# Attention scores by blocks of keys: one merged list of 64x64 matmuls, split additions, and a reordered head of the cycle

## The chip, the cores and the metric

The kernel runs on 1 core of one Trainium2 chip. Times are device microseconds of one execution of the whole program. Before the change three runs gave a median of 1027.56 us (1027.11 to 1027.65).

## What is computed

There are B = 64 sequences of N = 128 tokens with 512 channels. Each goes through one attention layer with 16 query heads of 64 channels that share one head of keys and values, with a bias per head, a causal mask, a mask of valid keys and an extra null key; then an output projection, a layer norm, and the residual. Cut to what matters:

```python
xn = layernorm(x, g_in)
q = (xn @ Wq).reshape(b, n, H, DH).transpose(0, 2, 1, 3) * scale    # 16 heads of 64
k, v = split(xn @ Wkv)                                              # one head, plus a null key
sim = jnp.einsum('bhid,bjd->bhij', q, k) + bias
sim = jnp.where(causal_mask, neg, sim)      # query i sees the null key and the keys up to i
sim = jnp.where(mask_p, sim, neg)
out = jnp.einsum('bhij,bjd->bhid', jax.nn.softmax(sim), v)
y = x + layernorm(out.reshape(b, n, INNER) @ Wo, g_out)
```

All of it is in float32. Each float32 matmul shows as two records of loading weights and two of multiplying (two passes) in the trace.

## The kernel before, in words

**Stages and order.** The order of the work on all engines is written out by hand: a prologue, then `cycle(c)` for c = 1 to 29, then a tail. A cycle handles two sequences in each of several stages at once: for b0 = 2c and b1 = 2c+1 the softmax, for two later ones (by n0 = b0+2 and n1 = b0+3) the scores, for the two before (p = b0-2) the output projection. It also makes the queries of a later group of four sequences (`q_one`, `leaf`: products of a fast matrix multiplication whose parts are added in place), the keys and values (`kv_mm`), and norms. Each cycle ends with `region(c)` (L1057): the scores of n0 and n1, and then the weighted values of b0 and b1.

**Scores.** The 128 queries of a sequence are four blocks of 32. For all 16 heads, the rows of a score tile are 128 = 2 blocks x 2 sets of heads x 32 queries. The lower half (`hf` = 0) has blocks 0 and 1 and a row of 64 keys, the upper half (`hf` = 1) blocks 3 and 2 and a row of 128 keys. `heads` (L645) makes them of 64x64 matmuls, four at a time in the four quarters of TensorE: r is the half of the contracted rows (heads with even or odd number), i the half of the output rows (i = 0: block 0, or 3 in the upper half; i = 1: block 1, or 2). So one half with index i of the array does blocks 0 and 3, and the other one blocks 1 and 2. The weights of each matmul are 64 queries (64 columns), and the keys stream through: 64 in the lower half, 128 in the upper one, for both blocks alike, though block 0 needs only 32, block 1 64, block 2 96 and block 3 128. The causal mask does away with the rest.

**Banks.** The upper half of n0 goes to the PSUM tile `s` (`ps_s`), the lower halves of both to `a` and `c`, and the upper half of n1 to two `w` banks. The values of `region` use `s` again, with `X` and `Y`. In the next cycle `q_one(c, 1, 0)` and `q_one(c, 6, 0)` multiply into `a`, `q_one(c, 5, 0)` into `c`, and `leaf(c, 2, 0)` into `w`.

**After the scores.** `scores_add` (L682) adds each piece of scores to the tile `S[b]`, which holds bias and masks already (VectorE, seven additions for a pair: one of 1024 columns, four of 256, two of 512). Then come the maximum (`scores_max`), the exponentials (ScalarE), the sum's reciprocal, and the scaling (GpSimd).

**Head of a cycle.** ScalarE moves the values out of PSUM (`values_out`: pieces 0 and 2 of p, then of p+1, then 1 and 3 of both). `q_one(c, 1, 0)` multiplies into `a` and has ScalarE copy the result (`first_into`, L503); the product of `q_one(c, 6, 0)` adds to the same bank, and so waits for that copy.

Of the kernel before, what the change touches and what calls it, by code (L numbers as in the profile page):

```python
# [17 lines left out]
def kernel(  # L18
# [405 lines left out]
    def q_part(g, c, h):  # L424

        f = c % NF
        return qT[g, f // FH, h][:, f % FH, :, :, c // NF, :]
# [214 lines left out]
    KEYS = LK, UK  # L642
    WITH_NULL = slice(0, 1 + NL), slice(1 + NL, ROW)

    def heads(b, hf, to):  # L645
        g, t = divmod(b, GB)
        for f in range(NF):
            for r in range(2):
                rows = slice(r * DH, (r + 1) * DH)
                for i in range(2):  # L650
                    nc.tensor.matmul(  # L651
                        to[r][i * DH : (i + 1) * DH, f, :],
                        qT[g, f // FH, t // GH][
                            rows, f % FH, t % GH, NQ - 1 - i if hf else i
                        ],
                        kT[g][rows, 0 : NQ if hf else NQ // 2, t, :],
                        start=True,
                        stop=True,
                    )

    def scores_upper(b, pool, tags):
        if len(tags) == 1:
            ps = pool.tile([P, 2, NF, N], FP, tag=tags, name=f"ps_{b}_1")
            heads(b, 1, [ps[:, r] for r in range(2)])
            pss[b, 1] = [(slice(0, R8), ps)]
        else:
            ps = [pool.tile([P, NF, N], FP, tag=t, name=f"ps_{b}_1{r}") for r, t in enumerate(tags)]
            heads(b, 1, ps)
            pss[b, 1] = [(slice(r * NF, (r + 1) * NF), ps[r]) for r in range(2)]

    def scores_lower(bs):
        low = [
            ps_q.tile([P, 2, NF, NL], FP, tag="ac"[r], name=f"ps_{bs[0]}_0{r}")
            for r in range(2)
        ]
        for k, b in enumerate(bs):
            heads(b, 0, [low[r][:, k] for r in range(2)])
            pss[b, 0] = [(slice(r * NF, (r + 1) * NF), low[r][:, k]) for r in range(2)]

    pss = {}  # L680

    def scores_add(b, hf):  # L682
        for ks, ps in pss.pop((b, hf)):
            sv = S[b][:, ks, KEYS[hf]]
            if ks.stop - ks.start == R8:
                sv = sv.rearrange("p (r f) j -> p r f j", r=2)
            nc.vector.tensor_tensor(sv, ps, sv, ALU.add)  # L687

    def scores_max(b, hf):
        if hf == 0:  # L690
# [289 lines left out]
    def q_one(c, k, h):  # L980
        i = 2 * c + 4 + h
        g, f = divmod(i, GB)
        if g >= NG:
            return
        if k == 1 and f % FH == 0:
            q_tile(g, f // FH)
        if k == 1:
            product(g, f, 1, ps_q, "a")
            if c >= LEAF:
                first_into(g, f, 0)  # L990
            else:
                keep("a", "p1")
        elif k == 2:
            product(g, f, 2, ps_w, "w")
            q_out(g, f, lo_t, "w", "p1")
        elif k == 5:
            product(g, f, 5, ps_q, "c")
        elif k == 6:
            product(g, f, 6, ps_q, "a", start=False)
            if c >= LEAF:  # L1000
                first_into(g, f, 1)
            else:
                keep("a", "u2")
        elif k == 7:
            product(g, f, 7, ps_q, "a", start=False)
            if c >= LEAF:
                first_into(g, HC + f, 0)
                nc.vector.tensor_tensor(
                    q_part(g, HC + f, 1), by_block("c"), q_part(g, HC + f, 0), ALU.add
                )  # L1010
            else:
                keep("a", "u3")
                q_out(g, HC + f, hi_t, "c", "u3")
        elif k == 8:
            o = q_part(g, f, 1)
# [62 lines left out]
    def cycle(c):  # L1078
# [19 lines left out]
            scores_max(b1, 0)  # L1098
            scores_max(b1, 1)
        if pair:  # L1100
            values_out(p + 1, (0, 2))
        if fin:
            pair_pow(r)
        if soft:
# [2 lines left out]
            tokens_in(2)  # L1107
        if first and LEAF <= c and more:
            leaf_sums(c // 2 + 1, 3)
        q_one(c, 1, 0)  # L1110
        if fin:
            pair_nmr(r)
        q_one(c, 5, 0)
# [10 lines left out]
            q_one(c, 2, 0)  # L1124
        if c >= LEAF:
            leaf(c, 2, 0)
        if soft:
            exps(b0, 0, 0, 2)
        q_one(c, 6, 0)
        if soft:  # L1130
            exps(b0, 0, 2, 8)
        out_one(p, 1)
        if c % 2 and n0 < B:
            mask_neg(n0 // GB)
# [6 lines left out]
        q_one(c, 7, 0)  # L1141
        if first and LEAF <= c and more:
            leaf_sums(c // 2 + 1, 4)
        if c >= LEAF:
            q_one(c, 8, 0)
        out_one(p, 2)
        if soft:
            exps(b0, 1, 0, 6)
        if fin:
# [90 lines left out]
        if soft:  # L1240
            scale(b1, 1)
        if c >= LEAF:
            leaf(c, 4, 1)
            q_one(c, 8, 1)
        if c < LEAF:
            q_one(c, 3, 1)
        if soft:
# [393 lines left out]
```

## Time and profile before

| | |
|---|---|
| median of three runs | 1027.56 us |
| span of the profiled execution | 1024.9 us |
| TensorE busy with matmuls | 1013.0 us |
| VectorE busy | 852.5 us |
| GpSimd busy | 788.2 us |
| ScalarE busy | 642.8 us |
| a cycle from scores to scores | 31.03 us |

The time of the profiled execution itself isn't shown; its span is 2.66 us shorter than the median of the runs, and that much is taken to lie around the span in all that follows. In the profile PE is TensorE, PEld its loading of weights, DVE VectorE, ACT ScalarE, POOL GpSimd. A row of groups ends with busy time, mean length of one, and idle time ahead of it; a row in order of time begins with start and length. The granted clock of TensorE was 0.998 of full speed.

### The profile page before, as it was taken

How to read it: one execution, taken by the hardware profiler on the slowest of the kernel's cores; microseconds unless marked ns; L12 is line 12 of the kernel's file. 1: busy time of each engine (PE TensorE's matmuls, PEld its weight loads, DVE VectorE, ACT ScalarE, POOL GpSimd, SP SyncE). 2: the span in 40 equal slices, each digit the busy share in tenths (PEclk: the TensorE clock that was granted, in tenths of full speed). 3: DMA queues.
4: the chain of work that ended last, by engine and by line, in shares of the span. 5: the costliest groups of instructions: out<-in, count | busy, mean ns of one | idle time of the engine just before them, and what ended most of it. 6: DMA issues, size and time to landing. Idle time of an engine off the chain costs nothing. (4 is left out here: it accounts for less than half of the span.)

```text
span 1024.9 us, 31793 instructions
## 1 busy us (share of the span) xinstructions
PE 1013.0 (99%) x12104; PEld 900.7 (88%) x12104; DVE 852.5 (83%) x2000; ACT 642.8 (63%) x2742; POOL 788.2 (77%) x710
## 2 busy tenths in 40 slices
PE   9999999999999999999999999999999999999997
PEld 8888888888888889888889888889888898888876
DVE  6776887888888888888888878788888888878798
ACT  2655776555776556775556765557765567755591
POOL 3799959688696878959689596887968789596874
PEclk9999999999999999999999999999999999999999
DMA  7542350524315152241623505253151521402203
GB/s 212 165 125 55 104 135 26 158 64 135 107 43 152 49 158 84 93 118 32 171 71 106 135 23 158 64 140 101 46 152 46 157 85 73 111 25 67 84 2 104
DMA packets 70264, 100.91 MB, mean 98 GB/s; under 512 B 27744, under 2 KB 31328, under 8 KB 68320
## 3 DMA queue, kind: packets, MB, share of 16 engines
q1 hardware_dynamic: 69008, 97.83, 33.1%
q8 instruction: 96, 1.57, 0.7%
q10 hardware_dynamic: 1104, 1.05, 0.3%
q14 instruction: 56, 0.46, 0.2%
HBM read 63.19 MB, written 33.55 MB: 94 GB/s over the span
## 5 line engine op out<-in xcount | busy, mean ns | idle before, releaser
L701 ACT ACTIVATE s<-s,nmax 128x65 f32<-128x65 f32 (+1 forms) x1024 | 382.2, 413 | 3.5 <-DVE nmax L692 3.5
L701 ACT ACTIVATION_READ_ACCUMULATOR s<-s,nmax 128x1 f32 x1024 | 242.0, 236 | 0.0
L722 POOL TENSOR_TENSOR s<-s,rinv 128x1024 f32<-128x1024 f32 (+1 forms) x128 | 189.4, 1482 | 46.4 <-DVE rinv L718 46.4
L635 POOL TENSOR_TENSOR s<-biasp,mneg 128x1552 f32<-128x1552 f32 x64 | 205.0, 3224 | 2.0 <-DMA x<-in_x_dram 2.0
L810 ACT ACTIVATE oT<-poX,nv 128x256 f32<-128x256 f32 x58 | 27.5, 474 | 219.2 <-PE poX L770 113.0
L687 DVE TENSOR_TENSOR s<-ps,s 128x256 f32<-128x256 f32 (+2 forms) x224 | 120.0, 605 | 15.7 <-PE ps L651 15.2
L556 DVE TENSOR_TENSOR qT<-pl,qT 128x128 f32<-128x128 f32 (+1 forms) x420 | 122.4, 323 | 3.3 <-PE pl L553 3.3
L860 PE MATMUL pyX<-wo,oT 128*128 128x256 f32 x512 | 121.4, 380 | 0.0
L692 DVE TENSOR_REDUCE nmax<-s 128x8 f32<-128x520 f32 (+1 forms) x128 | 116.5, 949 | 0.1
L860 PE MATMUL pyX<-wT,oT 128*128 128x256 f32 x488 | 115.7, 380 | 0.7 <-POOL oT L843 0.7
L737 DVE STREAM_TRANSPOSE sb<-s 128x1536 f32<-128x1536 f32 x64 | 113.1, 1768 | 0.6 <-POOL s L722 0.6
L860 PEld LDWEIGHTS pyX<-wo,oT 128*128 128x128 f32 x512 | 97.0, 190 | 14.3 <-issue 0.9
L917 POOL TENSOR_TENSOR rstdo<-rstdo,nhalf 128x1 f32<-128x1 f32 x64 | 35.0, 548 | 91.5 <-DVE rstdo L913 91.5
L860 PEld LDWEIGHTS pyX<-wT,oT 128*128 128x128 f32 x488 | 88.4, 191 | 10.8 <-POOL oT L843 1.1
L651 PE MATMUL ps<-kT,qT 64*64 64x128 f32 (+1 forms) x4096 | 93.7, 246 | 0.4 <-issue 0.4
L651 PEld LDWEIGHTS ps<-kT,qT 64*64 64x64 f32 x4096 | 85.5, 134 | 5.5 <-issue 2.1
L770 PE MATMUL pos<-sb,vr 32*64 32x128 f32 (+1 forms) x1792 | 81.4, 321 | 0.0
L843 POOL TENSOR_TENSOR yS<-oT 128x512 f32<-128x512 f32 x32 | 40.8, 1274 | 45.4 <-ACT oT L810 42.0
L770 PE MATMUL poY<-sb,vr 32*64 32x128 f32 x720 | 74.6, 348 | 0.0
L770 PE MATMUL poX<-sb,vr 32*64 32x128 f32 x960 | 73.5, 299 | 0.0
L503 ACT COPY qT<-pa 128x256 f32<-128x256 f32 x168 | 68.2, 406 | 1.4 <-PE pa L597 1.4
L331 DVE STREAM_TRANSPOSE xb<-x 128x512 f32<-128x512 f32 x56 | 39.4, 705 | 34.1 <-ACT x L310 34.1
(150 smaller groups left out, 2545.6 us busy)
## 6 DMA issues: line engine op xcount, KB each, us to landing
res<-in_x_dram SPq DMA_DIRECT2D x64, 256.0 KB, 2.9
out_dram<-y SPq DMA_DIRECT2D x58, 256.0 KB, 2.1
x<-in_x_dram SPq DMA_DIRECT2D x224, 64.0 KB, 2.0
xd<-xb SPq DMA_DIRECT2D x14, 1024.0 KB, 4.3
xT<-xd SPq DMA_DIRECT2D x56, 256.0 KB, 5.4
vr<-vd SPq DMA_DIRECT2D x64, 128.0 KB, 3.3
x<-in_x_dram SPq DMA_DIRECT2D x8, 256.0 KB, 4.8
vd<-vt SPq DMA_DIRECT2D x32, 64.0 KB, 6.2
```

What stands on the lines that cost most here:

```text
L503: nc.scalar.copy(q_part(g, c, h), by_block("a"))
L556: nc.vector.tensor_tensor(o, p, o, ALU.add)
L635: nc.gpsimd.tensor_tensor(S[b], biasp, mneg[:, t].unsqueeze(1).broadcast_to([P, R8, ROW]), ALU.add,)
L651: nc.tensor.matmul(to[r][i * DH : (i + 1) * DH, f, :], qT[g, f // FH, t // GH][rows, f % FH, t % GH, NQ - 1 - i if hf else i], kT[g][rows, ...
L687: nc.vector.tensor_tensor(sv, ps, sv, ALU.add)
L692: nc.vector.tensor_reduce(nmax[b][:, hf], S[b][:, :, WITH_NULL[hf]], AX.X, ALU.max, negate=True)
L701: nc.scalar.activation(row, row, AF.Exp, bias=nmax[b][:, hf, k : k + 1], accum_out=rsum[b][:, hf, k : k + 1],)
L722: nc.gpsimd.tensor_tensor(sv, sv, rinvs.pop((b, hf)).unsqueeze(2).broadcast_to([P, R8, sv.shape[2]]), ALU.mult,)
L737: nc.vector.transpose(sb.rearrange("p j e q -> p e j q"), S[b][:, :, 1 : ROW - 1].rearrange("p e (j k) -> p e j k", k=Q),)
L770: nc.tensor.matmul(po[s][rows, half], vr[g][quad(s), j, t, :], sb[quad(s), slots, r * NF : (r + 1) * NF, :], start=start, stop=True, skip_ ...
L843: nc.gpsimd.tensor_tensor(o, l, m, op)
L860: nc.tensor.matmul(prod[key], h[:, c, :], w[:, c, :], start=(start and c == 0), stop=(c == HC - 1), skip_group_check=not start,)
```

## The change

**Scores.** Each block of 32 queries is multiplied with its own keys only: 32, 64, 96 and 128 instead of 64, 64, 128 and 128. The numbers of matmuls and of weight loads stay the same. In `region`, the banks of all four pieces are taken first, and one list for both sequences replaces four loops. `heads` sorts that list by the place that each matmul would begin at if one block of 32 keys took one unit of time, for each index i apart, so that matmuls of both i with different lengths stand beside each other. In the tail the pieces are still made one by one, with the new lengths.

**Additions.** Scores of keys that a block hasn't been multiplied with are no longer there to be added. So each addition is split in two: one over all 128 rows and the keys that both blocks have, one over the 64 rows of the longer block and its last 32 keys. Seven additions of a pair become fourteen, with as many columns in all.

**Head of the cycle.** From cycle 2 on, `q_one(c, 1, 0)`, and with it the copy out of `a`, stands ahead of `values_out(p + 1, (2,))`. The eight exponentials of `exps(b0, 0)` stand together behind `q_one(c, 6, 0)` (before: two ahead of it, six behind). Both additions out of bank `c` (`q_one(c, 7, 0)` and `q_one(c, 8, 0)`) stand behind `out_one(p, 2)`, and `q_one(c, 8, 1)` ahead of `leaf(c, 4, 1)`.

```diff
+    def heads(parts):
+        runs = []
+        for i in range(2):
+            at = 0
+            for b, hf, to in parts:
+                block = NQ - 1 - i if hf else i
+                for f in range(NF):
+                    runs.append((at, i, b, block, f, to))
+                    at += block + 1
+        for _, i, b, block, f, to in sorted(runs, key=lambda run: run[:2]):
+            g, t = divmod(b, GB)
+            for r in range(2):
+                rows = slice(r * DH, (r + 1) * DH)
+                nc.tensor.matmul(
+                    to[r][i * DH : (i + 1) * DH, f, 0 : (block + 1) * Q],
+                    qT[g, f // FH, t // GH][rows, f % FH, t % GH, block],
+                    kT[g][rows, 0 : block + 1, t, :],
+                    start=True,
+                    stop=True,
+                )
...
     def scores_add(b, hf):
+        first = KEYS[hf].start
+        ends = (Q, 2 * Q) if hf == 0 else (3 * Q, 4 * Q)
         for ks, ps in pss.pop((b, hf)):
...
+            for rows, lo, hi in (
+                (slice(0, P), 0, ends[0]),
+                (slice((1 - hf) * DH, (2 - hf) * DH), ends[0], ends[1]),
+            ):
+                sv = S[b][rows, ks, first + lo : first + hi]
...
+                nc.vector.tensor_tensor(sv, pv, sv, ALU.add)
...
     def region(c):
...
-            scores_upper(n0, ps_s, "s")
-            scores_lower((n0, n1))
-            scores_upper(n1, ps_w, "ww")
+            up0 = score_banks(n0, ps_s, "s")
+            low = lower_banks((n0, n1))
+            up1 = score_banks(n1, ps_w, "ww")
+            heads([(n0, 1, up0), (n0, 0, low[0]), (n1, 0, low[1]), (n1, 1, up1)])
...
         if pair:
-            values_out(p + 1, (0, 2))
+            values_out(p + 1, (0,))
+        early = c < LEAF or p < 0
+        if not early:
+            q_one(c, 1, 0)
+        if pair:
+            values_out(p + 1, (2,))
```

The three places that the prediction speaks of, as the built programs have them. On TensorE, the scores of sequences 14 and 15 began like this before (`ps_1` is the upper half of 14, `ps_00` and `ps_01` the lower halves; the sizes are rows x keys, and x8 means eight alike):

```order
L651 MATMUL ps_1_3279<-kT_1883,qT_0_1_2179 64x128 x8
L651 MATMUL ps_1_3279<-kT_1883,qT_1_1_2600 64x128 x8
L651 MATMUL ps_00_3296<-kT_1883,qT_0_1_2179 64x64 x2
L651 MATMUL ps_01_3297<-kT_1883,qT_0_1_2179 64x64 x2
L651 MATMUL ps_00_3296<-kT_1883,qT_0_1_2179 64x64 x2
```

and now begin like this, at the same place:

```order
L679 MATMUL ps_1_3328<-kT_1911,qT_0_1_2205 64x128 x2
L679 MATMUL ps_1_3328<-kT_1911,qT_0_1_2205 64x96 x4
L679 MATMUL ps_1_3328<-kT_1911,qT_0_1_2205 64x128 x2
L679 MATMUL ps_1_3328<-kT_1911,qT_1_1_2638 64x96 x2
L679 MATMUL ps_1_3328<-kT_1911,qT_1_1_2638 64x128 x2
L679 MATMUL ps_1_3328<-kT_1911,qT_1_1_2638 64x96 x2
L679 MATMUL ps_1_3328<-kT_1911,qT_1_1_2638 64x128 x2
L679 MATMUL ps_00_3329<-kT_1911,qT_0_1_2205 64x64
L679 MATMUL ps_01_3330<-kT_1911,qT_0_1_2205 64x64
L679 MATMUL ps_00_3329<-kT_1911,qT_0_1_2205 64x64
L679 MATMUL ps_01_3330<-kT_1911,qT_0_1_2205 64x64
L679 MATMUL ps_00_3329<-kT_1911,qT_0_1_2205 64x32
```

Before, the four quarters took turns with equal lengths. Now a pair (r = 0 and 1) of one index i follows a pair of the other or of the same, and lengths mix; the lower halves begin while block 3 of the upper one still runs.

On ScalarE, the head of cycle 6 was this before (`oT` from `poX`, `poY` and `pos` are pieces of `values_out`, the copy of `pa` is `first_into`):

```order
L810 ACTIVATE oT_2996<-poX_2918,nv_87 128x2x4x32
L810 ACTIVATE oT_2996<-poY_2919,nv_87 128x2x4x32
L810 ACTIVATE oT_3002<-poX_2918,nv_87 128x2x4x32
L810 ACTIVATE oT_3002<-poY_2919,nv_87 128x2x4x32
L503 COPY qT_0_0_3013<-pa_0_1_3015 128x8x32
```

and is this now:

```order
L832 ACTIVATE oT_3045<-poX_2960,nv_87 128x2x4x32
L832 ACTIVATE oT_3045<-poY_2961,nv_87 128x2x4x32
L832 ACTIVATE oT_3051<-poX_2960,nv_87 128x2x4x32
L503 COPY qT_0_0_3053<-pa_0_1_3055 128x8x32
L832 ACTIVATE oT_3051<-poY_2961,nv_87 128x2x4x32
```

The copy of `pa` has moved from the fifth place to the fourth.

On VectorE, the additions for sequence 14 and the first of 15 were:

```order
L687 TENSOR_TENSOR s_3241<-ps_1_3279,s_3241 128x8x128
L687 TENSOR_TENSOR s_3241<-ps_00_3296,s_3241 128x4x64
L687 TENSOR_TENSOR s_3241<-ps_01_3297,s_3241 128x4x64
L687 TENSOR_TENSOR s_3253<-ps_00_3296,s_3253 128x4x64
L687 TENSOR_TENSOR s_3253<-ps_01_3297,s_3253 128x4x64
```

and are now:

```order
L709 TENSOR_TENSOR s_3290<-ps_1_3328,s_3290 128x8x96
L709 TENSOR_TENSOR s_3290<-ps_1_3328,s_3290 64x8x32
L709 TENSOR_TENSOR s_3290<-ps_00_3329,s_3290 128x4x32
L709 TENSOR_TENSOR s_3290<-ps_00_3329,s_3290 64x4x32
L709 TENSOR_TENSOR s_3290<-ps_01_3330,s_3290 128x4x32
L709 TENSOR_TENSOR s_3290<-ps_01_3330,s_3290 64x4x32
```

Each addition has become a wide one and a narrow one, in the old order. The built program has two waits of TensorE for its own earlier matmuls in each cycle that weren't there: at the first values that go into `s`, and at `leaf(c, 2, 0)`.

More of the change, by code (lines that the diff above doesn't have):

```diff
@@ L643, with score_banks, lower_banks @@
     WITH_NULL = slice(0, 1 + NL), slice(1 + NL, ROW)
[L645 to L661, printed above, removed]
+    pss = {}
+    def score_banks(b, pool, tags):
         if len(tags) == 1:
             ps = pool.tile([P, 2, NF, N], FP, tag=tags, name=f"ps_{b}_1")
-            heads(b, 1, [ps[:, r] for r in range(2)])
             pss[b, 1] = [(slice(0, R8), ps)]
[L666 to L671, printed above, removed]
+            return [ps[:, r] for r in range(2)]
+        ps = [pool.tile([P, NF, N], FP, tag=t, name=f"ps_{b}_1{r}") for r, t in enumerate(tags)]
+        pss[b, 1] = [(slice(r * NF, (r + 1) * NF), ps[r]) for r in range(2)]
+        return ps
+    def lower_banks(bs):
         low = [
@@ L1014, in q_one @@
         elif k == 8:
+            nc.vector.tensor_tensor(
+                q_part(g, HC + f, 1), by_block("c"), q_part(g, HC + f, 0), ALU.add
+            )
             o = q_part(g, f, 1)
@@ L1109, in cycle @@
             leaf_sums(c // 2 + 1, 3)
-        q_one(c, 1, 0)
+        if early:
+            q_one(c, 1, 0)
         if fin:
@@ L1242, in cycle @@
         if c >= LEAF:
+            q_one(c, 8, 1)
             leaf(c, 4, 1)
-            q_one(c, 8, 1)
         if c < LEAF:
```

26 lines of the change are left out of this document (13 added, 13 removed).

## The prediction, made before the changed kernel ran

> **What bounds the kernel now.** I read the page's busy times first, then the stretches of one cycle, then single rows.
>
> ```profile
> span 1024.9 us, 31793 instructions
> PE 1013.0 (99%) x12104; PEld 900.7 (88%) x12104; DVE 852.5 (83%) x2000; ACT 642.8 (63%) x2742; POOL 788.2 (77%) x710
> ```
>
> TensorE has work in 99% of the span, so a gain must shorten its own work or a gap in it; other engines matter only where they make it wait. The span lies 2.66 us under the median of 1027.56; I sum against 1024.9 and add 2.66. A measurement of this kernel can tell about 0.2% (2.1 us) from no change. One cycle in three stretches, scores, values and the rest (each row: stretch, its length, TensorE busy and its matmuls, granted clock, DMA share, GB/s):
>
> ```profile
> 499.07:501.91 2.84, 2.84 (x130) 1.00 0.51 119
> 501.91:504.36 2.45, 2.45 (x116) 1.00 0.88 224
> 504.36:530.10 25.74, 25.74 (x145) 1.00 0.40 113
> ```
>
> The change touches the first, and the beginning of the third.
>
> **The scores: fewer keys.** The scores of that cycle again, cut where the rows change from 128 keys to 64 and back (the counts include matmuls that run across an edge):
>
> ```profile
> 499.07:499.99 0.92, 0.92 (x32) 1.00 0.31 80
> 499.99:500.92 0.93, 0.93 (x72) 1.00 0.60 176
> 500.92:501.91 0.99, 0.99 (x46) 1.00 0.61 101
> ```
>
> In the middle each quarter of the array makes 8 matmuls of two passes: 0.93 / 16 = 58 ns a pass. In the first part it makes 8 passes; without the 0.05 us that the first load of weights takes, 0.87 / 8 = 109 ns. What would a pass of 32 or 96 keys take? A plain run of larger matmuls separates streaming from loading:
>
> ```profile
> 519.33 1.89 PE L860 MATMUL pyY<-wT,yS 128*128 128x256 f32 x8
> 521.06 0.39 PE L553 MATMUL pl<-xS,wq 128*128 128x128 f32 x2
> 521.28 0.39 PE L553 MATMUL pl<-xT,wS 128*128 128x128 f32 x2
> ```
>
> From start to start, eight passes of 256 columns take 1.73 us (216 ns each), two of 128 take 0.22 (110): 0.83 ns a column and about 2.5 ns. A pass of 96 keys should take 82 ns. By that, one of 32 takes 29 ns, if nothing else limits it. But each pass has its own load of 64 columns of weights. The loads of the values (also 64 columns) show their length where nothing hides them, behind a drain:
>
> ```profile
> 501.91 0.13 PEld L770 LDWEIGHTS poX<-sb,vr 32*64 32x64 f32 x2 [0.17 <-issue]
> ...
> 501.96 0.14 PEld L770 LDWEIGHTS poX<-sb,vr 32*64 32x64 f32 x2
> ...
> 502.07 0.14 PEld L770 LDWEIGHTS poX<-sb,vr 32*64 32x64 f32 x2
> ```
>
> The second load on the same part of the array starts 0.05 to 0.06 us after the first: a load occupies it that long. The third comes 0.11 later, with the next pass of 128: a load begins when the pass before it begins, and hides behind it. So a pass takes the longer of stream and load, and at 64 keys both are about equal (53 + 2.5 against 55). With 32 keys the load remains. I take **58 ns for a pass of 32 keys**, as for 64; the other end is 29.
>
> Now the sum by index i, since each half of the array has its own chain. For a pair of sequences, i = 0 has 16 passes of block 3 and 16 of block 0: 16 x 109 + 16 x 58 = 2.67 us, before and after alike. i = 1 has 16 of block 2 and 16 of block 1: 16 x 82 + 16 x 58 = 2.24 instead of 2.67. The values need the whole array, so the longer chain counts: **nothing gained**, where 31 merged lists would have given 31 x 0.43 = 13 us if block 0 had been cheap.
>
> By the Trainium skill (TensorEngine Tiling (Array Packing), Instruction Overhead) a matmul of free size 1 takes as long as one of about 60, which here would make 32 keys cost what 64 do, by another mechanism. No run here shows fewer than 64 keys; by that rule the gain is nothing too.
>
> The merged order lets quarters drift apart. In the values, where lengths are mixed as well, they do so freely:
>
> ```profile
> 502.20 0.38 PE L770 MATMUL poY<-sb,vr 32*64 32x256 f32 x2
> ...
> 502.40 0.29 PE L770 MATMUL poX<-sb,vr 32*64 32x128 f32 x2
> ...
> 502.42 0.38 PE L770 MATMUL poY<-sb,vr 32*64 32x256 f32 x2
> ```
>
> The last row is the second pass of the matmul in the first row; the `poX` between them stands behind both in the program and begins before. Still, the values cost 2.45 us, while one part's own chain (12 passes of 109, 4 of 216, 0.05 for the first load, 0.1 for the change of layout, as between 500.92 + 0.87 and 501.91) sums to 2.32: mixing costs up to 0.13 there. For the scores I take 0.016 a list, 31 x 0.016 = **+0.5 us**, between 0 and 0.13 (4.0 us).
>
> **The head of the cycle.** First an odd cycle, then an even one:
>
> ```profile
> 506.19 0.39 PE L553 MATMUL pl<-xT,wq 128*128 128x128 f32 x2
> 506.44 1.13 PE L597 MATMUL pa<-xS,wS 128*128 128x256 f32 x4
> 507.41 1.89 PE L860 MATMUL pyX<-wo,oT 128*128 128x256 f32 x8
> ```
>
> ```profile
> 537.22 0.38 PE L553 MATMUL pl<-xT,wq 128*128 128x128 f32 x2
> 537.57 1.10 PE L597 MATMUL pa<-xS,wS 128*128 128x256 f32 x4
> 538.51 1.68 PE L860 MATMUL pyX<-wo,oT 128*128 128x256 f32 x7
> ```
>
> Two passes of `pl` end at 506.19 + 0.22 = 506.41, but `pa` begins at 506.44; and its four passes take 0.97 to the next row instead of 4 x 0.216 = 0.86, because the first load isn't hidden. Together 0.14 us lost; in the even cycle 0.13 + 0.08 = 0.20. That it is so in every cycle shows in the groups:
>
> ```profile
> L597 PE MATMUL pa<-xS,wq 128*128 128x256 f32 x256 | 65.8, 380 | 0.0
> ...
> L597 PE MATMUL pa<-xS,wS 128*128 128x256 f32 x240 | 64.2, 390 | 0.5 <-ACT qT L503 0.5
> ```
>
> The waiting group (which also has products elsewhere in the cycle) is 10 ns longer in the mean, 240 x 0.010 = 2.4 us, as 14 x 0.10 + 14 x 0.08 would give. What TensorE waits for is on ScalarE:
>
> ```profile
> 505.29 0.47 ACT L810 ACTIVATE oT<-poX,nv 128x256 f32<-128x256 f32 x1
> 505.65 0.48 ACT L810 ACTIVATE oT<-poY,nv 128x256 f32<-128x256 f32 x1
> 506.00 0.39 ACT L503 COPY qT<-pa 128x256 f32<-128x256 f32 x1
> ```
>
> The copy out of `a` ends at 506.39, and `pa` follows 0.05 later. The change puts the copy one place ahead, to 505.65. Its data are there: the product before it in `a` begins at 504.36 and takes 1.13,
>
> ```profile
> 504.36 1.13 PE L597 MATMUL pa<-xT,wq 128*128 128x256 f32 x4
> ```
>
> so it ends at 505.49. The copy then ends at 506.04, ahead of 506.30, where the load for `pa` could start. The wait goes whole; next on this path is only TensorE's own `pl`. In 28 cycles (2 to 29): 14 x 0.14 + 14 x 0.20 = **-4.7 us**. What is displaced, `values_out(p + 1, (2,))`, comes one copy later, and all six pieces and two copies still end where they did. The exponentials that stood ahead of the second copy follow it, with the same work in sum.
>
> **The additions.** VectorE's costs, by size, then the seven of that cycle together:
>
> ```profile
> L687 DVE TENSOR_TENSOR s<-ps,s 128x256 f32<-128x256 f32 x128 | 45.2, 413 | 0.0
> L687 DVE TENSOR_TENSOR s<-ps,s 128x512 f32<-128x512 f32 x64 | 40.8, 678 | 0.0
> L687 DVE TENSOR_TENSOR s<-ps,s 128x1024 f32<-128x1024 f32 x32 | 39.2, 1224 | 15.7 <-PE ps L651 15.2
> ```
>
> ```profile
> 500.32 3.74 DVE L687 TENSOR_TENSOR s<-ps,s 128x1024 f32<-128x1024 f32 x7
> ```
>
> About 1.05 ns a column and 145 ns fixed. The seven sum to 4.23 but take 3.74, so neighbours overlap by 0.08, and a further addition costs 0.065 net. Rows don't matter to an engine that counts columns:
>
> ```profile
> L331 DVE STREAM_TRANSPOSE xb<-x 128x512 f32<-128x512 f32 x56 | 39.4, 705 | 34.1 <-ACT x L310 34.1
> L384 DVE STREAM_TRANSPOSE vt<-kT 64x512 f32<-64x512 f32 x16 | 11.3, 709 | 0.5
> ```
>
> Seven more: +0.45 us a pair, 14 us of VectorE in all. Who waits? The values into `s` need the first addition: it ends at 500.32 + 1.22 = 501.54, now 501.60, and they begin at 501.91. `a` must be free at 504.36; its last reader now ends near 503. The exponentials wait for the maxima:
>
> ```profile
> 504.98 2.42 DVE L692 TENSOR_REDUCE nmax<-s 128x8 f32<-128x520 f32 x3
> 507.69 0.41 ACT L701 ACTIVATE s<-s,nmax 128x65 f32<-128x65 f32 x1
> ```
>
> They end at 507.40, now near 507.85, and ScalarE now gets there near 508.0, behind the second copy. So in the cycles the cover holds, and I count nothing; without it each cycle would lose up to 0.06 at the values (1.8 us). The two added waits on TensorE are for matmuls finished long before, and both instructions wait longer for VectorE anyway; queued behind them are the values and the head's products. In the tail the cover is thin:
>
> ```profile
> 964.00:985.00 21.00, 20.06 (x470) 16.42 (x469) 19.90 (x40) 14.72 (x81) 15.99 (x10) 1.00 0.01 3
> ```
>
> VectorE (the third pair, 19.90) is busy in 95% of it, so its seven further additions count: **+0.4**. The moved additions out of `c` and the leaf cost nothing: `c` is multiplied into again only in the cycle's second half.
>
> **Sum:** -4.7 + 0.5 + 0.4 = -3.8: span 1021.1, time **1023.8 us**.
>
> **Rivals.**
>
> Cheap short keys: a pass of 32 takes 29 ns, because a load is faster than it looks beside others. For: 64 keys could be bound by either. Against: the 0.055 between two loads. The scores then end 0.43 earlier, but the values meet the first addition (501.60), so about 0.28 of it counts: 30 x 0.28 = 8.4 more, 1015.
>
> The order costs more than it gives: the queue is held up by a matmul whose quarter is busy, where two of the same index follow each other. In the list this idles i = 0 at four places, for two matmuls of 96 keys (0.165 each) and two of 64 (0.116): at most 0.56 a list. Half of it, 31 x 0.28 = 8.7, gives 1027.56 - 4.3 + 8.7 = 1032, **slower**. It cancels the gain from 0.14 a list on. Against it: the `poX` above, which passed a waiting `poY`. By the Trainium skill (TensorE: Matmul & The Clock Gate, Packing small matmuls) matmuls start and end strictly in program order, which would bring this about; the `poX` row at 502.40 speaks against it. At 0.1 to 0.17 a list, the result is no change: about 1027.5.
>
> The head's wait stays, because another wait stands behind the copy: 1027.56 + 0.9 = 1028.5, no change.
>
> **How the numbers follow.** Forecast (1022.9 to 1025.4) 0.60; cheap keys 0.13; the order cancels the gain 0.11; the wait stays 0.06; the order makes it slower 0.10. Faster by over 0.2%: 0.60 + 0.13 = 0.73; same 0.11 + 0.06 = 0.17; slower 0.10. The range reaches from 1015, the middle of the cheap case, to 1029.0, past the two cases without change; left out are the slower case and half of the cheap one.
>
> **What would show it.** The stretch from scores to values stays near 2.84 us, 32-key rows start every 58 ns on a quarter, and i = 1 is done 0.4 earlier than i = 0. `pa<-xS,wS` follows `pl` without a gap, at 0.22. A stretch of 2.4 to 2.6 proves the forecast wrong on the loads; one over 2.95, wrong on the order; a gap ahead of `pa`, wrong on the head.

## The result, and the profile after

| | before | after |
|---|---|---|
| median | 1027.49 us (four runs) | 1044.38 us (four runs, 1043.92 to 1044.82) |
| span of the profiled execution | 1024.9 us | 1042.4 us |
| a cycle from scores to scores (odd, even) | 31.03, 31.09 us | 31.61, 31.55 us |

The ratio is 1.0165 (95% interval 1.0153 to 1.0178): 16.9 us **slower** (1.65%), where 3.8 faster was forecast. The first part of the page:

```profile
span 1042.4 us, 32021 instructions
PE 1017.4 (98%) x12104; PEld 896.5 (86%) x12104; DVE 891.6 (86%) x2224; ACT 647.8 (62%) x2742; POOL 786.8 (75%) x710
```

Of the 17.5 us in the span, TensorE's busy time has 4.4; the rest is time in which it stands still. VectorE's busy time grew by 39 us, where the prediction had 14. The same cycle as before in its three stretches (length, TensorE, its loads, VectorE, ScalarE, GpSimd, granted clock, DMA share, GB/s):

```profile
505.98:508.80 2.82, 2.82 (x129) 2.65 (x128) 2.74 (x8) 0.00 (x0) 2.13 (x1) 1.00 0.72 174
508.80:511.26 2.46, 2.46 (x117) 2.05 (x113) 2.33 (x8) 0.00 (x0) 0.00 (x0) 1.00 0.81 180
511.26:537.60 26.34, 25.87 (x144) 22.92 (x139) 23.36 (x60) 20.35 (x86) 17.23 (x14) 1.00 0.40 109
```

Scores and values are as long as before (2.84 and 2.45). The third stretch is 0.60 longer, and TensorE is idle in it for 0.47. In order of time, TensorE first shows the head, and then the wait:

```profile
513.09 0.38 PE L553 MATMUL pl<-xT,wq 128*128 128x128 f32 x2
513.31 1.03 PE L597 MATMUL pa<-xS,wS 128*128 128x256 f32 x4
514.17 1.89 PE L882 MATMUL pyX<-wo,oT 128*128 128x256 f32 x8
515.90 1.03 PE L597 MATMUL pa<-xS,wq 128*128 128x256 f32 x4
516.76 1.89 PE L882 MATMUL pyw<-wo,oT 128*128 128x256 f32 x8
519.12 1.13 PE L597 MATMUL pa<-xT,wq 128*128 128x256 f32 x4 [0.47 <-ACT qT L503]
```

`pa<-xS,wS` follows `pl` at 0.22 and takes 0.86 to the next row: the stall at the head is gone, as forecast. But the `pa` of 519.12 (`q_one(c, 1, 1)`) should start 1.73 behind 516.76, at 518.49. It waits for the copy that empties bank `a` after `q_one(c, 7, 0)`. In the groups of waits this is new, and so is the one of ScalarE behind it (time in all, times, longest):

```profile
ACT s L723 <- DVE nmax L714: 21.7, 29, 3.7
PEld pa L597 <- ACT qT L503: 21.6, 28, 1.0
PE pa L597 <- ACT qT L503: 10.7, 26, 0.8
```

On ScalarE the copy at 518.70 stands behind the eight exponentials, and they began late:

```profile
514.59 0.43 ACT L503 COPY qT<-pa 128x256 f32<-128x256 f32 x1
515.77 0.35 ACT L723 ACTIVATE s<-s,nmax 128x65 f32<-128x65 f32 x1 [0.75 <-DVE nmax L714]
...
518.45 0.35 ACT L915 COPY kyp<-pyX 128x256 f32<-128x256 f32 x1
518.70 0.37 ACT L503 COPY qT<-pa 128x256 f32<-128x256 f32 x1
```

And on VectorE the maxima come after fourteen additions that take 5.08 us together (before: seven, 3.74):

```profile
507.23 5.08 DVE L709 TENSOR_TENSOR s<-ps,s 128x768 f32<-128x768 f32 x14
512.24 0.67 DVE L931 BATCH_NORM_STATS2 sto<-y 128x6 f32<-128x512 f32 x1
...
513.23 2.42 DVE L714 TENSOR_REDUCE nmax<-s 128x8 f32<-128x520 f32 x3
```

So the chain reads: additions 1.34 us longer, maximum 1.34 later, ScalarE idle 0.75, copy late, `pa` 0.63 later than it should start, and its first load laid bare (its four passes take 0.97 to the next row instead of 0.86). Together this is about 0.7 us in nearly every one of 28 cycles. Why do seven further additions cost 1.34 and not 0.45? Two neighbours in the lower half, with 128 columns each:

```profile
508.72 0.29 DVE L709 TENSOR_TENSOR s<-ps,s 64x128 f32<-64x128 f32 x1
...
509.03 0.29 DVE L709 TENSOR_TENSOR s<-ps,s 128x128 f32<-128x128 f32 x1
```

They start 0.31 apart, longer than one of them lasts: they don't overlap at all. The two leaf additions of 128 columns (L556) just ahead of the scores start 0.198 apart, at a length of 0.28. The eight additions of the lower halves start 0.29 to 0.33 apart, mostly 0.305. Eight at 0.305 instead of 0.198 are 0.86 us, nearly all of the 0.89 between 1.34 and the 0.45 that was forecast.

### The profile page after: what moved, and what is told of

Its sections match the earlier page's. It is cut to its first block, busy times and chain, and to the rows that moved or that the text cites. A ratio compares the mean times of both kernels' runs of the same rounds, so it can differ in the third digit from the quotient of the medians.

```text
span 1042.4 us, 32021 instructions
## 1 busy us (share of the span) xinstructions
PE 1017.4 (98%) x12104; PEld 896.5 (86%) x12104; DVE 891.6 (86%) x2224; ACT 647.8 (62%) x2742; POOL 786.8 (75%) x710
## 5 line engine op out<-in xcount | busy, mean ns | idle before, releaser
L723 ACT ACTIVATE s<-s,nmax 128x65 f32<-128x65 f32 (+1 forms) x1024 | 372.7, 373 | 21.7 <-DVE nmax L714 21.7
L723 ACT ACTIVATION_READ_ACCUMULATOR s<-s,nmax 128x1 f32 x1024 | 201.4, 197 | 0.0
L709 DVE TENSOR_TENSOR s<-ps,s 128x128 f32<-128x128 f32 (+2 forms) x448 | 158.0, 380 | 19.6 <-PE ps L679 14.6
L556 DVE TENSOR_TENSOR qT<-pl,qT 128x128 f32<-128x128 f32 (+1 forms) x420 | 122.5, 323 | 2.6 <-PE pl L553 1.8
L882 PEld LDWEIGHTS pyX<-wT,oT 128*128 128x128 f32 x488 | 88.3, 190 | 10.9 <-POOL oT L865 1.1
L679 PE MATMUL ps<-kT,qT 64*64 64x32 f32 (+3 forms) x4096 | 93.4, 241 | 0.1
L597 PE MATMUL pa<-xT,wq 128*128 128x256 f32 x240 | 67.5, 404 | 10.1 <-ACT qT L503 9.9
L597 PEld LDWEIGHTS pa<-xT,wq 128*128 128x128 f32 x240 | 40.9, 189 | 35.7 <-ACT qT L503 20.6
```

The costliest lines, as they stand in the source:

```text
L556: nc.vector.tensor_tensor(o, p, o, ALU.add)
L597: nc.tensor.matmul(prod[tag], w[:, kc, f * P : (f + 1) * P], t[:, :, kc, :], start=(start and kc == 0), stop=(kc == HK - 1), skip_group_ch ...
L679: nc.tensor.matmul(to[r][i * DH : (i + 1) * DH, f, 0 : (block + 1) * Q], qT[g, f // FH, t // GH][rows, f % FH, t % GH, block], kT[g][rows, ...
L709: nc.vector.tensor_tensor(sv, pv, sv, ALU.add)
L723: nc.scalar.activation(row, row, AF.Exp, bias=nmax[b][:, hf, k : k + 1], accum_out=rsum[b][:, hf, k : k + 1],)
L882: nc.tensor.matmul(prod[key], h[:, c, :], w[:, c, :], start=(start and c == 0), stop=(c == HC - 1), skip_group_check=not start,)
```

## Experiments

**Theory A**: the fourteen additions delay the maximum, and through ScalarE's copy TensorE. **Theory B**: ScalarE's new order (eight exponentials in one piece) makes the copy late. For the price of an addition, **C**: the rows 64 to 127 alone cost it; **D**: any short addition does.

**e1_whole_adds.** In the changed kernel:

```diff
-                    to[r][i * DH : (i + 1) * DH, f, 0 : (block + 1) * Q],
+                    to[r][i * DH : (i + 1) * DH, f, :],
-                    kT[g][rows, 0 : block + 1, t, :],
+                    kT[g][rows, 0 : NQ if hf else NQ // 2, t, :],
...
+            nc.vector.tensor_tensor(sv, ps, sv, ALU.add)
```

> The changed kernel with whole additions again (seven a pair); so that they have something to add, every block is multiplied with the keys it had before (64 or 128), in the merged list. Theory A: the fourteen additions hold VectorE 1.34 us longer than the seven (5.08 against 3.74), the maximum of b0 comes that much later, ScalarE waits 0.75 us for it, and the copy out of bank a (L503, behind the exponentials) is late for TensorE. Then the wait of TensorE for that copy and that of ScalarE for the maximum both go, and only the gain of the head is left: 1027.5 - 4.7 = 1022.8, between 1021.5 and 1025. Theory B: it is the new order on ScalarE, eight exponentials in one piece ahead of that copy, which makes it late; then the wait stays and it takes 1039 to 1045. The stretch from scores to values stays near 2.84 if a pass of 32 keys costs what one of 64 does; were the short keys worth something, it would grow over the 2.83 of the changed kernel.

Measured 1033.73 us, ratio 1.0062 (1.0045 to 1.0078). Both waits are gone, so A holds against B; but the time is 10.9 above the expected 1022.8. The scores show most of it:

```profile
471.16:474.24 3.08, 3.08 (x129) 2.91 (x129) 2.31 (x6) 0.00 (x0) 3.08 (x2) 1.00 0.04 8
```

3.08 instead of 2.84, 31 times 0.24 = 7.5 us. Another 2.5 us are stalls in the values, of the kind that g1 and j1 show below. The list was still sorted for the short lengths while the matmuls had the old ones: the experiment changed two things. It is no proof that the short keys are worth 0.24; it prices a list whose order doesn't fit its lengths.

**e2_split_adds** and **e3_head_only** take one part of the change each, on the kernel before:

```diff
 e2:   scores_add as in the change
 e3:
-            values_out(p + 1, (0, 2))
+            values_out(p + 1, (0,))
+        early = c < LEAF or p < 0
+        if not early:
+            q_one(c, 1, 0)
+        if pair:
+            values_out(p + 1, (2,))
...
-            exps(b0, 0, 0, 2)
         q_one(c, 6, 0)
-            exps(b0, 0, 2, 8)
+            exps(b0, 0)
```

> The kernel before with one thing of the change, the additions split in two (scores, keys and the head as before). Theory A: the maximum comes 1.3 us later, to 508.75 on the clock of the profile before; there two exponentials stand ahead of the second copy out of a, so this copy ends at 508.77 + 1.18 = 509.95 instead of 508.77, while TensorE needs it at 509.14: a wait of 0.86 and 0.1 of a load laid bare, 28 times, and the 4.7 us of the head are lost besides: 1027.5 + 27 = 1054, between 1047 and 1058, slower than the whole change. The next copy is then not late any more. Theory B: within 2 us of 1027.5, since ScalarE's order is the old one.

> The kernel before with the new head alone: the product and its copy one place ahead, and the eight exponentials together behind the second copy; scores, additions and the additions out of bank c as before. Theory A: the gain of the head and nothing against it, 1027.5 - 4.7 = 1022.8, between 1021.5 and 1025, as in e1_whole_adds within 1.5 us (the merged list is worth nothing). Theory B: 1039 to 1045.

e2 took 1055.14 us (ratio 1.0270, 1.0255 to 1.0285), e3 1023.37 (0.9960, 0.9946 to 0.9975). Both are as A has them, and B is out: with the new order on ScalarE and whole additions the kernel is faster than before, and with the old order and split additions it is slower than the whole change. In e2 the wait stands one product earlier, ahead of `q_one(c, 7, 0)`, since there the copy before it is behind two exponentials:

```profile
490.24 1.13 PE L597 MATMUL pa<-xS,wq 128*128 128x256 f32 x4 [0.57 <-ACT qT L503]
```

In e3 one cycle is 30.90 us, 0.13 under the odd and 0.19 under the even one of before, which are the two stalls of the prediction:

```profile
466.91:469.75 2.84, 2.84 (x130) 2.67 (x129) 2.08 (x6) 0.00 (x0) 2.84 (x2) 1.00 0.01 3
469.75:472.20 2.45, 2.45 (x116) 2.04 (x112) 2.45 (x6) 0.00 (x0) 2.45 (x3) 1.00 0.02 7
472.20:497.81 25.61, 25.61 (x144) 23.01 (x139) 21.15 (x53) 20.17 (x86) 23.98 (x28) 1.00 0.27 94
```

**e4_all_rows**: e1 with the additions split again, the second part over all rows.

```diff
-                (slice((1 - hf) * DH, (2 - hf) * DH), ends[0], ends[1]),
+                (slice(0, P), ends[0], ends[1]),
```

> As e1_whole_adds, but with fourteen additions: split at the same columns as in the change, both parts over all 128 rows. In the change, the eight additions of the lower halves start 0.305 us apart although they have 128 columns, for which 0.198 would be expected (two leaf additions of 128 columns stand 0.198 apart). Theory C: the 0.107 is the price of going to the rows 64 to 127 alone and back; the additions for the upper halves, whose short part has the rows 0 to 63, don't pay it (0.198). Then the lower additions here stand 0.198 apart, all fourteen take 4.1 us, ScalarE doesn't wait, and the time is 1023 to 1025. Theory D: it is the price of several short additions behind each other, whatever their rows; then they stand 0.305 apart here too, and the time is 1042 to 1045.

It took 1032.33 us (1.0048, 1.0033 to 1.0063), above the 1023 to 1025 expected. The badly sorted list of e1 is in it too, so the absolute time says little, but beside e1 the seven further additions cost nothing. The eight of 128 columns start 0.198 apart. That speaks for C; f1 to f3 repeat it without the list.

**f1_head_split, f2_head_split_all_rows, f3_head_split_low_rows**: e3 with `scores_add` of the change, and its second part in three forms.

```diff
 f1:            (slice((1 - hf) * DH, (2 - hf) * DH), ends[0], ends[1])
 f2:            (slice(0, P), ends[0], ends[1])
 f3:            (slice(0, DH), ends[0], ends[1])
```

> The kernel before with the new head and the additions split as in the change; scores by the four old loops, over the keys of before. So the change without its merged list. Theory A (the additions alone make the loss): the wait of TensorE for the copy out of a as in the change, 17 us on top of 1023.4: 1040.5, and the values without the stalls of the change (2.8 us there, in which TensorE waits for nothing that the profile shows), so 1039 to 1043. If the list had a part in the wait: below 1035.

> As f1_head_split, but the second part of each addition has all 128 rows: as many additions, and more rows and elements in all. Theory C (rows 64 to 127 alone are what costs): the additions of 128 columns start 0.198 apart, the fourteen take 4.1 us instead of 5.0, ScalarE finds its maximum in time, and the time is that of e3_head_only, 1023.4, up to 0.6 more for the tail: 1022.8 to 1025. Theory D' (fourteen additions are too many, whatever each costs): the maximum comes 0.45 us later and some of it reaches TensorE, 1026 to 1032.

> As f1_head_split, but the second part of each addition, in the lower halves too, goes over the rows 0 to 63 instead of 64 to 127: same sizes (64 x 128), same order, other rows. The scores of the rows 64 to 127 for the last 32 keys of the lower half are left out of the sum by that. Theory C: 0.198 to 0.21 apart, time 1022.8 to 1025. If any addition over half of the rows costs it: 0.305 apart as in the change, 1039 to 1043.

f1 took 1047.63 us (1.0195, 1.0178 to 1.0212), f2 1023.48 (0.9961, 0.9946 to 0.9976), f3 1023.32 (0.9959, 0.9944 to 0.9974). f1 and f3 differ in nothing but the rows of four small additions a pair: 24.3 us. (f3 leaves the scores of rows 64 to 127 for the last 32 keys of the lower half out of the sum; the amount of work is the same.) The group of these additions in f1, and ScalarE's wait:

```profile
L697 DVE TENSOR_TENSOR s<-ps,s 64x128 f32<-64x128 f32 x192 | 55.2, 287 | 1.7
```

```profile
ACT s L711 <- DVE nmax L702: 23.6, 30, 3.8
```

and in f3:

```profile
L697 DVE TENSOR_TENSOR s<-ps,s 64x128 f32<-64x128 f32 x192 | 52.4, 273 | 0.0
```

```profile
ACT s L711 <- DVE nmax L702: 3.6, 2, 3.4
```

The length hardly tells it (287 against 273 ns); the price is in the overlap that is lost. In f2 two neighbours together take this long:

```profile
500.36 0.47 DVE L697 TENSOR_TENSOR s<-ps,s 128x128 f32<-128x128 f32 x2
```

that is 0.198 + 0.278. All fourteen take 4.19 us in f2 and f3, and 5.08 in f1. Beside the 3.74 of the seven, that is 0.45 for seven further ones that start at row 0. So **C** is shown, and D is out. The Trainium skill has a rule for this (VectorE: DVE Perf Modes, Two Vector instructions with no wait between them): an instruction is held until all earlier ones of VectorE have finished if its data in SBUF or PSUM start in another group of 32 partitions than those of the last instruction that used that memory. By that, an addition on the rows 64 to 127 is held, and so is the next one on all rows, while one on the rows 0 to 63 isn't. The traces agree in each of the three forms, at 0.305 against 0.198 us; the prediction could have drawn on that rule and didn't.

f1 is 3.2 us above the whole change, and there I had expected less (1039 to 1043). TensorE loses a little more in each cycle (0.04 ahead of `pkv`, and 0.10 because the first load of `pkv` is laid bare). f1 lacks the moved additions out of bank `c`; that these make the difference when VectorE is late was not tried by itself.

**h3_cut_by_rows** asks how the price goes with size: e3, with the lower additions cut into two halves of rows.

```diff
-            nc.vector.tensor_tensor(sv, ps, sv, ALU.add)
+            for rows in (slice(0, DH), slice(DH, P)) if hf == 0 else (slice(0, P),):
```

> As e3_head_only, but the four additions of the lower halves are cut by rows: 0 to 63 and 64 to 127, all 64 keys each (256 columns). It asks how the price of the upper rows goes with size. In the change a 64-row addition beside them doesn't overlap its neighbours: it starts 13 ns behind the end of the one before (0.305 apart at a length of 0.291). By that the ones here stand 0.42 to 0.43 apart instead of 0.331 (lengths 0.413), 8 of them 3.4 us; the maximum comes 2.1 us later than in e3_head_only, ScalarE waits about 1.5 us for it, and TensorE over 1 us in each cycle: 1050 to 1070. If the price is only in starting small ones, they stand 0.331 apart, the additions take 5.0 us, as in f1_head_split, and the time is near its 1047.

The eight stand 0.42 to 0.46 apart; a single run took 1074.17 us. Without the hold they would stand 0.331 apart, so that is a loss of 0.09 to 0.13 us at each change of rows, as with 128 columns (0.29 to 0.33 for 0.198): from 128 to 256 columns it doesn't grow. The wait of the maximum:

```profile
ACT s L711 <- DVE nmax L702: 49.5, 31, 4.2
```

The time is above the expected range (1050 to 1070): behind the pieces on the rows 64 to 127 the next one starts 0.44 to 0.46 later, where 0.42 to 0.43 had been counted. That is some 0.1 us more a cycle, 3 us in all (an estimate from these distances).

**g1_max_first** leaves the slow additions and moves what waits for them.

```diff
+            scores_max(b0, 0)
             scores_max(b1, 0)
             scores_max(b1, 1)
...
-            scores_max(b0, 0)
```

> The whole change, with one line moved: the maximum of b0's lower half ahead of the two maxima of b1 on VectorE. The slow additions stay. The maximum that ScalarE waits for comes 1.74 us earlier (0.60 and 1.14 of the two others). Theory A: the wait of ScalarE for the maximum goes (21.7 us in 29 waits in the change), and with it that of TensorE for the copy: 1044.3 - 17.1 = 1027.2, between 1025 and 1030. If the copy is late for ScalarE's own work, it stays at 1042 to 1045.

It took 1045.91 us (1.0185, 1.0160 to 1.0209): a miss by 18.7 us, though the mechanism is as expected. ScalarE's wait for the maximum is down to 4.4 us, and the copy is in time. But other waits took the place:

```profile
PEld pos L792 <- issue: 13.5, 12, 2.1
...
PEld pyX L882 <- POOL oT L865: 7.3, 13, 1.1
```

The second is a sum of GpSimd that comes late (ahead of `out_one(p, 7)`, some 0.4 us in most even cycles). The first is no engine: in the middle of the values, TensorE stands still with nothing to wait for:

```profile
509.09 0.32 PE L792 MATMUL pos<-sb,vr 32*64 32x128 f32 x2 [1.18 <-issue]
```

and the stretch in which that falls has the DMA engines full (share 1.09):

```profile
507.45:511.37 3.92, 2.74 (x115) 2.20 (x112) 3.79 (x12) 0.00 (x0) 0.00 (x0) 1.00 1.09 226
```

In the DMA records, one queue carries nothing but 96 blocks of 16 KB. That they are TensorE's instructions is inferred: the profile has about 24,700 records of TensorE, some 257 to a block. One block is fetched at the beginning of the scores: in the odd cycles of e3 from 0.1 us ahead of them (median), in 0.9 to 1.5 us. In this cycle of g1 it was fetched from 1.87 us behind their start. Of the eight cycles whose values take over 1 us too long, seven have the fetch at 1.4 to 2.2 and the eighth at 0.57, but for 2.48 us. The stall begins at the same matmul each time, 3.29 us behind the start of the scores, and ends 1.4 to 1.6 us behind the end of that fetch, so a late block is what TensorE stands still for. All eight are odd cycles, in which the transfers of tokens fall into the scores. That the traffic makes the fetch late is inferred from that and was not tried by itself.

**h1_lower_whole** repairs the change where C says: the lower halves get their 64 keys back and whole additions.

```diff
-                    to[r][i * DH : (i + 1) * DH, f, 0 : (block + 1) * Q],
+                    to[r][i * DH : (i + 1) * DH, f, 0 : (max(block, 1) + 1) * Q],
...
-                (slice((1 - hf) * DH, (2 - hf) * DH), ends[0], ends[1]),
-            ):
+                (slice(0, DH), ends[0], ends[1]),
+            ) if hf else ((slice(0, P), 0, ends[1]),):
```

> The whole change, repaired at one place: in the lower halves both blocks are multiplied with 64 keys again (block 0 too), and so their four additions are whole; the upper halves keep their short keys (96 and 128) and split additions, whose short parts have the rows 0 to 63. Ten additions, none on the rows 64 to 127 alone. If a pass of 32 keys costs as much as one of 64, the stretch from scores to values stays at 2.83. Theory C: additions 3.85 us, no wait for the maximum, time that of e3_head_only, less 0.4 for the scores, and 0 to 3 us for stalls of the values: 1023 to 1026. If the loss lies in the merged list or in the moved additions out of bank c: over 1035.

It took 1026.93 us (1.0001, 0.9988 to 1.0014): 17.5 us of the loss are gone, and the scores take 2.83 with 32 keys or 64 for block 0. 3.5 us to e3 are left, and its ten runs lie 6.5 us apart (1024.93 to 1031.42; e3's within 1.2). The values hold it: 72.1 us in 28 regions together (e3: 69.2), by the same stall as in g1, in a few cycles. The fetch begins 0.18 us behind the start of the scores.

**h4_no_list, j1_moved_c, j2_c_back** ask which part brings it.

```diff
 h4 (h1 with the old loops):
-        for _, i, b, block, f, to in sorted(runs, key=lambda run: run[:2]):
+        for b, hf, to in parts:
+            for f in range(NF):
+                for r in range(2):
+                    for i in range(2):
 j1 (on e3; j2 on h1 the other way):
-                nc.vector.tensor_tensor(
-                    q_part(g, HC + f, 1), by_block("c"), q_part(g, HC + f, 0), ALU.add
-                )
         elif k == 8:
+            nc.vector.tensor_tensor(
+                q_part(g, HC + f, 1), by_block("c"), q_part(g, HC + f, 0), ALU.add
+            )
...
-            q_one(c, 8, 0)
         out_one(p, 2)
+            q_one(c, 8, 0)
...
-            leaf(c, 4, 1)
             q_one(c, 8, 1)
+            leaf(c, 4, 1)
```

> h1_lower_whole with the matmuls of the scores in the old order (piece by piece, no merged list), everything else as there: short keys in the upper halves, their additions split, the new head, the additions out of bank c moved. It asks what makes h1_lower_whole slower than e3_head_only by 3.5 us, which lies in the values: 2.9 us of stalls there, in which TensorE waits for nothing that the profile shows while its next block of instructions is fetched 0.3 us later than in e3_head_only. If the list is the cause: the values take 2.453 us again in nearly every cycle (69.2 us in the regions of cycles 2 to 29 instead of 72.1), scores 2.84, time 1023 to 1024.5. If it is the moved or the split additions on VectorE, which change when transfers start: 71 us and more, 1026 to 1027.

> e3_head_only with one further thing of the change: the additions out of bank c moved as there (both behind out_one(p, 2), and q_one(c, 8, 1) ahead of leaf(c, 4, 1)). If they are what brings the stalls in the values (with another wait on TensorE, which moves its instructions in their blocks, and the fetch of the next block 0.2 us behind the start of the scores instead of 0.1 ahead): the time is 1026 to 1028, fetch at +0.2. If not: 1023 to 1024, fetch at -0.1.

> h1_lower_whole with the additions out of bank c back in their old places: short keys in the upper halves, merged list, ten additions, new head. If the moved additions bring the stalls: 1022.5 to 1024, values clean (2.453 us), fetch at -0.1. If it is the banks taken ahead or the short keys: 1026 to 1028, fetch at +0.2.

h4 took 1027.31 us (1.0007, 0.9996 to 1.0018), values 72.1: the list isn't it. j1 took 1029.14 (1.0019, 1.0009 to 1.0029), 5.8 above e3 by the moved additions alone, with the stalls and the fetch at +0.22:

```profile
130.95 0.32 PE L770 MATMUL pos<-sb,vr 32*64 32x128 f32 x2 [0.72 <-issue]
```

j2 took **1023.11** (0.9961, 0.9946 to 0.9975), fetch at -0.10, values 69.3. So the moved additions out of bank `c` cost 3.8 to 5.8 us, by stalls of TensorE's instructions. Of the other kernels, those with the moved additions have the fetch at +0.17 to +0.25 (median of the odd cycles; g1: 1.4), those without at -0.09 to -0.18.

How can a move on VectorE delay this fetch by 0.3 us? TensorE's records are the same 768 in a cycle of e3 and of j1, with waits at the same places. But with `q_one(c, 8, 1)` ahead of `leaf(c, 4, 1)`, the last leaf additions ahead of the scores come later. In e3 (scores from 497.81) and in j1 (from 500.06):

```profile
495.80 0.72 DVE L556 TENSOR_TENSOR qT<-pl,qT 128x256 f32<-128x256 f32 x2
```

```profile
498.39 0.71 DVE L556 TENSOR_TENSOR qT<-pl,qT 128x256 f32<-128x256 f32 x2
```

They end 1.29 us ahead of the scores in e3, and 0.96 in j1. The load `pl<-xS,wq` of TensorE waits for VectorE there. No engine stands still for it. But in every kernel except g1 the fetch begins 1.1 to 1.2 us behind the end of these additions (median), so the 0.3 us are those by which they moved. That this wait holds the fetch is inferred from that; no run moves it alone.

j2 is the version to keep, with e3 level with it.

**k1_half_weights** asks what makes a pass of 32 keys cost 58 ns.

```diff
+                cols = DH if block else DH // 2
-                    to[r][i * DH : (i + 1) * DH, f, 0 : (block + 1) * Q],
-                    qT[g, f // FH, t // GH][rows, f % FH, t % GH, block],
+                    to[r][i * DH : i * DH + cols, f, 0 : (block + 1) * Q],
+                    qT[g, f // FH, t // GH][rows, f % FH, t % GH, block, 0 : cols // Q],
```

> The change with half of the weight columns in the matmuls of block 0 (32 instead of 64); one head of two is left out of block 0's scores by that, and the additions of the lower half go over the rows 0 to 31 (32 keys) and 64 to 127 (64 keys). The question is what makes a pass of 32 keys take 58 ns. Loads (the prediction): a load of 32 columns takes half of 55 ns, so these passes start 29 to 36 ns apart. Something else, the same for every small pass: they stay at 58. The stretch is then 2.83 in the second case; in the first the chain of i = 0 falls from 2.67 to 2.2 and the values wait for the other half (2.24) or for the first addition, 2.4 to 2.65.

Within a run of such passes the starts are 32 ns apart (500.688, 500.720 and 500.752 us in one cycle), and two loads on the same part 28: by that, it is the load of 64 columns that holds a 32-key pass at 58. The expected shorter stretch did not come: it is 4.25 us, and the single run took 1099.07 us.

```profile
499.14:503.39 4.25, 4.25 (x129) 3.59 (x128) 2.27 (x7) 0.00 (x0) 4.25 (x3) 1.00 0.02 4
```

At each change between tiles of 64x64 and 64x32, ten in a list, the next load starts 0.12 to 0.15 us behind the last matmul's start, and between two changes only one of the two halves works: TensorE empties. The Trainium skill (TensorEngine Tiling (Array Packing), Tiling Modes) says that a change of the tiling mode drains TensorE; here that has a price. I had not counted it.

## Why the prediction was wrong

**The sum by runs.** The head, e3 against before, -3.9; short keys in the upper halves, the list and three additions, j2 against e3, -0.3; the moved additions out of `c`, h1 against j2, +3.8; short lower keys, whose additions lie on the rows 64 to 127, the change against h1, +17.5. Together +17.1, measured +16.9. Each step begins where the last one ends, so this sum must close and proves nothing by itself. The traces split the 17.5 us of the span on their own: the third stretches of 28 cycles +12.7 (17.1 longer than in e3, where the head alone brings -4.4), the values +3.2, the scores -0.4, what comes behind the last values +1.5, and the rest 0.5.

**The step that failed** is the price of an addition: "a further addition costs 0.065 net", and behind it "Rows don't matter to an engine that counts columns". The rows quoted for that compare lengths, 705 ns on 128 rows and 709 on 64, and the hold is not in the length. The 64 rows of that transpose (L384) are the rows 64 to 127, and in order of time the profile before shows what it does to its neighbours:

```profile
499.07 0.48 DVE L556 TENSOR_TENSOR qT<-pl,qT 128x128 f32<-128x128 f32 x2
499.58 0.71 DVE L384 STREAM_TRANSPOSE vt<-kT 64x512 f32<-64x512 f32 x1
500.32 3.74 DVE L687 TENSOR_TENSOR s<-ps,s 128x1024 f32<-128x1024 f32 x7
```

It starts 0.03 us behind the end of the additions ahead of it, while those two overlap by 0.08; the row behind it also starts 0.03 after its end (that one waits for TensorE too). Measured, seven further additions cost 1.34 us a pair, not 0.45; the hold at the rows 64 to 127 is nearly all of the 0.89 between. For additions that start at row 0 the price was right: 0.45 in f2 and f3. "In the cycles the cover holds" was then wrong by its input: with fourteen additions at the price forecast (f2), the maximum comes in time, and the time is 1023.48. The cover had about 0.6 us (1.34 less the 0.75 that ScalarE waits; the prediction's own 508.0 less 507.40 is the same), and the prediction did not say what an addition may cost before it is gone. "+0.4" in the tail failed by the same price: there the change is 1.2 us longer than e3, f2 by less than 0.1.

**The second step that failed** is "The moved additions out of `c` and the leaf cost nothing". No engine stands still for them, but the fetch of TensorE's instructions came later: 3.8 to 5.8 us.

**The loads** were right. In the change, 32-key passes start 58 ns apart on a quarter (507.046, 507.104, 507.162 us), the stretch is 2.83, and e3 and j2, without and with short keys, are level. The rival of cheap short keys is out. "i = 1 is done 0.4 earlier than i = 0" was wrong: the last passes start at 508.57 and 508.60. The half with i = 1 gets ahead in its first 64-key passes (58 ns apart) and is then held to between 106 and 127 ns, so here it didn't run far ahead in the list.

**The order** cost nothing (the scores are 0.014 us a list shorter, where 0.016 longer was forecast). But an order can cost: in e1, where the lengths don't fit it, a list loses 0.24 us. The rival that had the change slower had it so by the order; the time came out on its side by another cause.

**The head** was right: `pa` at 0.22 behind `pl`, 0.13 and 0.19 us a cycle, 28 cycles 4.5 us; e3 gained 3.9 in all. In its profile the last values, ahead of the tail, stall for 0.7 us longer than before.

## What to carry to other kernels

An instruction that is split is priced by its start-to-start time beside its new neighbours, on the rows that it will have, not by columns or length alone; here the same additions on the rows 0 to 63 or on all rows were free, and on the rows 64 to 127 they cost 24 us. Where a cover is counted on, write down how long it is and from which price of the step it is gone. And a wait that is taken away at one place is worth only what the next one behind it leaves: look at GpSimd's sums and at the fetch of instructions too.

## What the runs showed of the hardware

VectorE: neighbours with the same first row overlap by 0.08 us (128 columns start 0.198 apart at a length of 0.278, 256 columns 0.331 at 0.413); behind a change between row 0 and row 64 they don't overlap (0.29 to 0.33 and 0.42 to 0.46). TensorE: behind a change of tile shape between 64x64 and 64x32 the next load starts 0.12 to 0.15 us after the last matmul's start; loads of 32 columns of weights follow each other in 28 ns, and loads of 64 hold a pass at 58. TensorE's instructions come over the DMA engines (inferred above), 16 KB at a time in 0.9 to 2.5 us; scores and values use up about two such blocks in 5.3 us, and in g1, where a block came late in cycles with full data queues, the loads stood still for up to 2.1 us and the matmuls for up to 1.8.
